# A graph layer on one core: tiles in two stretches a pair, and node spans a pair later

## The chip, the cores and the metric

The kernel runs on one core of a Trainium2 chip. The metric is the device time of one execution in microseconds. The kernel before was timed in three runs: 3030.13, 3025.53 and 3028.81 us, a median of 3028.81.

## The reference

A layer of a graph network with 12,500 nodes of 32 features and 400,000 edges, sorted by their target node `dst`:

```python
h = relu(layernorm(x))
e = concat([h[src], h[dst], edge_attr])          # 96 features an edge
v = relu(e @ W1 + b1) @ W2 + b2                  # 96 -> 64 -> 32
cand = segment_max(v, dst, num_segments=12500)   # the largest v of each node's edges
out = x + maximum(cand, h)
```

All is float32.

## The kernel before

**Tiling.** The edges are cut into four stripes of 100,000; each stripe takes 32 of the 128 partitions. A stripe is cut into chunks of 512 edges, 196 chunks in all (`NCH`), so one chunk holds 4 x 512 edges. The main loop handles two chunks a turn, called a **pair** here: `for c in range(0, NCH, 2)`, with `a = c + 2` and `b = c + 3` the next two chunks, which are prepared while c and c + 1 are finished.

**A chunk.** The hidden layer is a sum of three products in PSUM (`ph`): the edges' own features (`edges_into`, from the load `ea`), the target nodes' part (`windows_into`, a small window `qw` of precomputed rows times a one-hot `of` that `window_hots` makes on ACT out of the load `db`), and the source nodes' part (`ht`, from `h[src]`).

Source rows come in two ways. Twelve of the sixteen groups of 128 rows of a chunk are fetched by indirect DMAs on POOL (`gather`, L159, one DMA a group), and DVE transposes them in four parts (`to_features(c, 0..3)`, L274). The other four groups are taken by TensorE out of a copy of all rows on chip (`tile(c, m)`, L256: 14 matmuls of 448 columns with a one-hot `hot`, then two DVE operations that pick the row, L260 and L261). `to_features(c, J)` transposes those. The one-hots `hot` of a chunk are made by DVE (`one_hots`, groups 0 to 4, L225) and ACT (`one_hots_act`, groups 5 and 6, L234 and L235) from the load `kb`; `mask_of` belongs to them.

After `ph` come the bias and relu on ACT (`hid`, L574), the second layer on PE (into `pv`, L591), and a running maximum along the edges on DVE (`sm`, a scan that starts anew at each node, L598; the load `pb` tells it where). The last edge of each node then holds the node's maximum. To bring these to memory, `leave_1` transposes a chunk's `sm` on PE (four matmuls, L500) and adds `b2` on DVE (`so`, L502); `lasts` makes a one-hot of the last edges on DVE (L492); `leave_2` multiplies both on PE (L510), copies the result to `wo` on ACT (L514), and SP stores four windows of 32 nodes (L518).

**Order.** The order of the instructions on SP, PE, DVE and ACT is that of the program, written out by hand. In a pair it is: tile(a,0); the `ht` matmuls; `hid`; tile(a,1) and tile(a,2), with the one-hots of b between them on DVE; `ea`, second layer and window matmuls; `leave_2` of the chunk c - 1; the two scans; tile(a,3); `leave_1(c)`; tile(b,0); `leave_2(c)`; tile(b,1); `leave_1(c + 1)`; tile(b,2), tile(b,3). So PE does the tiles in stretches of 3 (b,2, b,3 and the next a,0), 2, 1, 1 and 1.

**Loads.** Each fourth chunk `load` brings `ea` (1 MB, issued on SP), `db` (1 MB) and `pb` (0.5 MB, both issued on ACT) for four chunks; the pairs between bring `kb` on ACT. Each pair SP also issues eight small loads `qw`. Waits for PSUM: the tag `pv` has three buffers, which tiles, second layer, transposes and `leave_2` share in the order of the program.

After the loop the stores are read back, the maximum with `h` and the sum with `x` are made on DVE, and the result is stored.

Of the kernel before, what the change touches and what calls it, by code (L numbers as in the profile page):

```python
# [8 lines left out]
F32 = mybir.dt.float32  # L9
# [5 lines left out]
ALU = mybir.AluOpType  # L15
# [8 lines left out]
P = 128  # L24
N = 12500
E = 400000
D = 32
# [40 lines left out]
def gnn_kernel(ctx, tc, x, src, src_mm, src_t, dst, dst_ext, lo, lo_c, ends_b, edge_attr, weights, w1, w2, b2, out):  # L68
# [84 lines left out]
    def gather(c):  # L153
        n = min(K - MM * (c in MMC), (SE - c * C) // D)
        parts = []
        for k in range(0, n, SOME):
            parts.append(gathered.tile([P, SOME, D], F32, name="gh"))
            for i in range(min(SOME, n - k)):
                nc.gpsimd.indirect_dma_start(  # L159
                    out=parts[-1][:, i, :], out_offset=None, in_=h_d[:, :],  # L160
                    in_offset=bass.IndirectOffsetOnAxis(ap=src_i[:, c, k + i:k + i + 1], axis=0))
        return parts
# [82 lines left out]
    def tile(c, m):  # L245

        if c not in MMC:
            return
        if m == 0:
            mm_rows[c] = early.tile([P, MM, D], F32, name="gm", bufs=6)  # L250
        hot = hots[c]
        e = slice(m * P, (m + 1) * P)
        po = early_ps.tile([P, C], F32, name="pv", bufs=3)[:, :D * A0]
        for k in range(A1):
            for part in range(2):
                nc.tensor.matmul(po, hot[:, k, e], hs[:, part, k].rearrange("p f a -> p (f a)"),  # L256
                                 start=(k == 0 and part == 0), stop=(k == A1 - 1 and part == 1))
        of_group = po.rearrange("p (f a) -> p f a", a=A0)
        one = early.tile([P, D, A0], F32, name="one", bufs=2)
        nc.vector.tensor_tensor(one, of_group, masks[c][:, m, None, :].to_broadcast([P, D, A0]), op=ALU.mult)  # L260
        nc.vector.tensor_reduce(mm_rows[c][:, m, :], one, axis=AX.X, op=ALU.max)  # L261

    def to_features(c, part):

        if c >= NCH:
            return
        if c not in hts:
            hts[c] = early.tile([P, K, D], F32, name="ht", bufs=4)
        ht = hts[c]
        n = min(K - MM * (c in MMC), (SE - c * C) // D)  # L270
        if part < J:
            r = slice(part * SOME, min((part + 1) * SOME, n))
            if r.start < n:
                nc.vector.transpose(ht[:, r].rearrange("p k e -> p (k e)"),  # L274
                                    gh[c][part][:, :r.stop - r.start].rearrange("p k f -> p (k f)"))
# [31 lines left out]
    with tc.tile_pool(name="nodes", bufs=1) as pool, tc.tile_pool(name="nodes_ps", bufs=2, space=PSUM) as ps:  # L307
# [147 lines left out]
    with tc.tile_pool(name="edges", bufs=3) as pool, tc.tile_pool(name="edges_ps", bufs=1, space=PSUM) as ps:  # L455
# [46 lines left out]
            nc.vector.tensor_tensor(so, px, b2r[:, None, :].to_broadcast([P, J, P]), op=ALU.add)  # L502
            return so

        def leave_2(c, so, last):

            pw = early_ps.tile([P, C], F32, name="pv", bufs=3)[:, :2 * D]
            for j in range(J):
                for g in range(2):
                    nc.tensor.matmul(pw[g * 2 * W:(g + 1) * 2 * W],  # L510
                                     last[:, j, 2 * g:2 * g + 2].rearrange("p s w -> p (s w)"),
                                     so[:, j, g * 2 * D:(g + 1) * 2 * D], start=(j == 0), stop=(j == J - 1))
            wo = pool.tile([P, 2 * D], F32, name="wo")
            nc.scalar.activation(wo, pw, AF.Copy)  # L514
            _, base = windows.pop(c)
            for s in range(NS):
                g = slice(s * W, (s + 1) * W)
                nc.sync.dma_start(top_d[s % 2][bass.ds(base[s], W), :], wo[g, s % 2 * D:(s % 2 + 1) * D])  # L518

        def into_ph(ph, pairs, start, stop):  # L520
            for s in range(NS):
# [25 lines left out]
        windows_into(0, ph)  # L547
        raw_2(3)
        raw_3(3)
        sm = None  # L550
        leave = lambda: None
        for c in range(0, NCH, 2):
            a, b = c + 2, c + 3
            for k in range(a, min(a + 2, NCH)):
                gh[k] = gather(k)
            load_keys(a + 2)
            for k in range(c + AHEAD, min(c + AHEAD + 2, NCH)):
                load(k)
            b_next = (c + 3 * AHEAD) // BLOCK
            if c % LOAD and b_next < NB and b_next not in ats and b_next not in loaded_b:  # L560
                load_block(b_next)

            if a == NCH - 2:
                nc.gpsimd.tensor_tensor(again.rearrange("p (g a) f -> p g a f", a=A0),
                                        hs[:, 0].rearrange("p g f a -> p g a f"),
                                        hs[:, 1].rearrange("p g f a -> p g a f"), op=ALU.add)
            tile(a, 0)
            to_features(a, 0)
            ht = [hts.pop(c + x).rearrange("p k e -> p (k e)") for x in range(2)]
            into_ph(ph, [(w1a, ht[x]) for x in range(2)], False, True)  # L570
            hid = []
            for s in range(NS):
                hid.append(pool.tile([P, C], F32, name="hid", bufs=6))
                nc.scalar.activation(hid[s], ph[s], AF.Relu, bias=b1c)  # L574
            for k in range(a, min(a + 2, NCH)):
                window_hots(k)
            one_hots_act(b)
            one_hots(b, 0, 2)
            tile(a, 1)
            to_features(a, 1)  # L580
            one_hots(b, 2, BY_ACT.start)
            mask_of(b)
            tile(a, 2)
            to_features(a, 2)
            last = [lasts(c)]
            ph = edges_into(a)
            pv = [early_ps.tile([P, C], F32, name="pv", bufs=3) for x in range(2)]
            for s in range(NS):
                for x in range(2):
                    g = slice(x * HID, (x + 1) * HID)  # L590
                    nc.tensor.matmul(pv[x][s * D:(s + 1) * D], w2x[g], hid[s][g], start=True, stop=True)  # L591
            windows_into(a, ph)
            leave()
            sms = []
            for x in range(2):
                before = -LOW if sm is None else sm[:, C - 1:C]
                sm = pool.tile([P, C], F32, name="sm", bufs=3)
                nc.vector.tensor_tensor_scan(sm, loaded.pop(c + x)[2], pv[x], before, op0=ALU.add, op1=ALU.max)  # L598
                sms.append(sm)
            tile(a, 3)  # L600
            one_hots_act(a + 2)
            to_features(a, 3)
            to_features(a, J)
            so = leave_1(c, sms[0])
            last.append(lasts(c + 1))
            tile(b, 0)
            to_features(b, 0)
            one_hots(a + 2, 0, 2)
            leave_2(c, so, last[0])
            tile(b, 1)  # L610
            to_features(b, 1)
            so = leave_1(c + 1, sms[1])
            one_hots(a + 2, 2, BY_ACT.start)
            mask_of(a + 2)
            tile(b, 2)
            to_features(b, 2)
            if c == 2 * AHEAD:
                places(FIRST, len(MMC))
            if (c + 4) % BLOCK == 0 and (c + 4) // BLOCK < NB:
                make_block((c + 4) // BLOCK)  # L620
            tile(b, 3)
# [12 lines left out]
            leave = lambda c=c + 1, so=so, last=last[1]: leave_2(c, so, last)  # L634
        leave()


    with tc.tile_pool(name="out", bufs=1) as pool:
# [152 lines left out]
```

## Time and profile before

| | |
|---|---|
| median of 3 runs | 3028.81 us |
| the profiled execution | 3030.95 us, its span 3029.2 us |
| PE matmul busy | 2886.8 us (95%) |
| POOL busy | 2242.3 us (74%), 2321 gathers of 944 ns |
| DVE busy | 2237.1 us (74%) |
| ACT busy | 1084.6 us (36%) |
| granted TensorE clock | 0.982 |

The profile is of one execution. A row of the timeline has the start and the length in us, the engine, the line, the operation, what it writes and reads, and how many were merged; in brackets stand the idle time of the engine before it and what ended it. A row of a group has the count, then the busy time in us and the mean of one in ns, then the idle time of the engine just before these instructions and what ended most of it. An engine's name with a q is its sequencer, which issues DMAs. Issuing a DMA isn't counted as busy, except for the indirect ones on POOL.

### The profile page before, as it was taken

What the parts mean: (1) busy time and instruction counts of PE and PEld (TensorE: products, weight loads), DVE (VectorE), ACT (ScalarE), POOL (GpSimd) and SP (SyncE); (2) the same over time, 40 slices, a digit from 0 to 9 for tenths busy, and PEclk for the clock granted to TensorE, in tenths of its full rate; (3) what the DMA queues carried; (4) which work ended last, traced back from release to release, by engine and by line L of the source; (5) the groups of instructions that cost most, each with busy time, mean ns of one, the idle gap of its engine ahead of it and who ended that gap; (6) DMA issues with size and microseconds to landing.
All of it is one profiled execution on the core that took longest, in us unless ns stands there. A gap on an engine that the chain in (4) does not pass through costs nothing. (4 is left out here: it accounts for less than half of the span.)

```text
span 3029.2 us, 58575 instructions
## 1 busy us (share of the span) xinstructions
PE 2886.8 (95%) x21077; PEld 2303.5 (76%) x21077; DVE 2237.1 (74%) x3865; ACT 1084.6 (36%) x1791; POOL 2242.3 (74%) x2372
## 2 busy tenths in 40 slices
PE   2899999999999999999999999999999999999995
PEld 1678787787878878787878787878787878787774
DVE  5578777777777777777777777777777777777775
ACT  3343433334343343434343434343434343334341
POOL 7777777777777777777777777777777777777774
PEclk7899999999999999999999999999999999999997
DMA  5432233233324323332333233223332332223322
GB/s 200 120 84 71 63 81 79 63 66 84 73 59 86 77 60 75 81 70 60 67 83 72 60 69 84 69 63 66 84 73 59 70 83 70 63 66 82 70 54 72
DMA packets 189045, 229.43 MB, mean 76 GB/s; under 512 B 117821, under 2 KB 160461, under 8 KB 175950
## 3 DMA queue, kind: packets, MB, share of 16 engines
q10 hardware_dynamic: 26692, 110.28, 12.1%
q1 hardware_dynamic: 86762, 76.66, 10.9%
q0 software_dynamic: 75296, 38.70, 8.9%
q8 instruction: 166, 2.72, 0.4%
q14 instruction: 129, 1.06, 0.1%
HBM read 211.54 MB, written 13.85 MB: 74 GB/s over the span
## 5 line engine op out<-in xcount | busy, mean ns | idle before, releaser
L159 POOL DMA_INDIRECT gh<-h_d,src_i x2321 | 2192.1, 944 | 740.6 <-issue 527.7
L256 PE MATMUL pv<-hs,hot 128*128 128x448 f32 x10808 | 2304.3, 368 | 40.8 <-DVE sm L598 40.8
L256 PEld LDWEIGHTS pv<-hs,hot 128*128 128x128 f32 x10808 | 1999.4, 189 | 266.3 <-issue 69.0
L260 DVE TENSOR_TENSOR one<-pv,mask 128x448 f32<-128x448 f32 x772 | 478.1, 619 | 629.4 <-PE pv L256 629.4
L574 ACT ACTIVATE hid<-ph,wt 128x512 f32<-128x512 f32 x392 | 237.2, 688 | 1240.7 <-PE ph L524 1099.6
L225 DVE TENSOR_TENSOR hot<-kb,consts 128x1024 fp32r<-128x1024 f16 (+2 forms) x385 | 561.0, 1457 | 0.0
L261 DVE TENSOR_REDUCE gm<-one 128x32 f32<-128x448 f32 x772 | 478.6, 620 | 26.6
L235 ACT ACTIVATE hot<-away,ones 128x512 fp32r<-128x512 f32 x386 | 279.3, 723 | 274.6 <-issue 261.7
L234 ACT ACTIVATE away<-kb,key_n 128x512 f32<-128x512 f16 x386 | 273.6, 709 | 0.0
L598 DVE TENSOR_TENSOR_SCAN sm<-pb,sm,pv 128x512 f32<-128x512 bf16 x195 | 247.6, 1270 | 17.3 <-PE pv L591 5.9
L274 DVE STREAM_TRANSPOSE ht<-gh 128x96 f32<-128x96 f32 x774 | 208.4, 269 | 58.7 <-DMA gh<-h_d,src_i 58.2
L510 PEld LDWEIGHTS pv<-so,last 128*64 128x64 f32 x3136 | 108.1, 138 | 114.5 <-DVE last L492 86.1
L514 ACT ACTIVATE wo<-pv 128x64 f32<-128x64 f32 x196 | 44.0, 224 | 344.1 <-PE pv L510 307.1
L486 ACT ACTIVATE of<-db,below 128x512 f32<-128x512 int32 x196 | 141.5, 722 | 24.8 <-DMA db<-in_dst_ext 24.8
L487 ACT ACTIVATE of<-of,ones 128x512 f32<-128x512 f32 x196 | 141.9, 724 | 6.4
L510 PE MATMUL pv<-so,last 128*64 128x64 f32 x3136 | 135.2, 229 | 5.2 <-DVE so L502 4.0
L524 PE MATMUL ph<-of,qw 32*64 32x512 f32 x1568 | 114.1, 617 | 21.1 <-DMA qw<-q_d 21.1
L524 PE MATMUL ph<-ea,wt 32*64 32x512 f32 x1568 | 110.0, 617 | 21.5 <-DMA qw<-q_d 21.5
L492 DVE TENSOR_TENSOR last<-consts,at 128x512 f32<-128x512 f32 x196 | 129.9, 663 | 0.0
L502 DVE TENSOR_TENSOR so<-pv,wt 128x512 f32<-128x512 f32 x196 | 127.8, 652 | 2.2 <-PE pv L500 2.2
L500 PE MATMUL pv<-ident,sm 128*128 128x128 f32 x784 | 118.1, 273 | 0.8 <-DVE sm L598 0.8
L524 PE MATMUL ph<-ht,wt 32*64 32x512 f32 x1568 | 116.0, 617 | 0.0
(80 smaller groups left out, 590.7 us busy)
## 6 DMA issues: line engine op xcount, KB each, us to landing
ea<-in_edge_attr SPq DMA_DIRECT2D x49, 1024.0 KB
db<-in_dst_ext ACTq DMA_DIRECT2D x48, 1024.0 KB
gh<-h_d,src_i POOLq DMA_INDIRECT x2321
pb<-pen_d ACTq DMA_DIRECT2D x48, 512.0 KB
kb<-key_d ACTq DMA_DIRECT2D x47, 512.0 KB
qw<-q_d SPq DMA_DIRECT2D x784, 8.0 KB
top_d<-wo SPq DMA_DIRECT2D x784, 4.0 KB
top_d<-zero ACTq DMA_DIRECT2D x2, 1568.0 KB
```

Of the source, the lines that this page charges most:

```text
L159: nc.gpsimd.indirect_dma_start(out=parts[-1][:, i, :], out_offset=None, in_=h_d[:, :], in_offset=bass.IndirectOffsetOnAxis(ap=src_i[:, c, ...
L225: nc.vector.tensor_tensor(hot_of(c)[:, start:stop], keys[c][:, None, :].to_broadcast([P, n, MM * P]), key_ps[:, start:stop, None].to_broad ...
L234: nc.scalar.activation(away, keys[c], AF.Square, bias=key_n[:, k:k + 1])
L235: nc.scalar.activation(hot_of(c)[:, k], away, AF.Relu, bias=ones, scale=-1.0)
L256: nc.tensor.matmul(po, hot[:, k, e], hs[:, part, k].rearrange("p f a -> p (f a)"), start=(k == 0 and part == 0), stop=(k == A1 - 1 and par ...
L260: nc.vector.tensor_tensor(one, of_group, masks[c][:, m, None, :].to_broadcast([P, D, A0]), op=ALU.mult)
L261: nc.vector.tensor_reduce(mm_rows[c][:, m, :], one, axis=AX.X, op=ALU.max)
L274: nc.vector.transpose(ht[:, r].rearrange("p k e -> p (k e)"), gh[c][part][:, :r.stop - r.start].rearrange("p k f -> p (k f)"))
L510: nc.tensor.matmul(pw[g * 2 * W:(g + 1) * 2 * W], last[:, j, 2 * g:2 * g + 2].rearrange("p s w -> p (s w)"), so[:, j, g * 2 * D:(g + 1) * ...
L524: nc.tensor.matmul(ph[s][x * HID:(x + 1) * HID], w[g], e[g], start=start, stop=stop)
L574: nc.scalar.activation(hid[s], ph[s], AF.Relu, bias=b1c)
L598: nc.vector.tensor_tensor_scan(sm, loaded.pop(c + x)[2], pv[x], before, op0=ALU.add, op1=ALU.max)
```

## The change

- The order of the tiles. `tile(a, 0)` is done at the end of the turn before. Behind the `ht` matmuls stands only tile(a,1); tile(a,2), tile(a,3), the four tiles of b and the next tile(a,0) follow the scans in one stretch. So there are two stretches, of 1 and of 7 tiles.
- `leave_1` and `leave_2` of the chunks c and c + 1 are done in the next turn: both transposes behind the `ht` matmuls, both products behind the window matmuls, in one PSUM tile with one copy `wo` and eight stores. After the loop the last two chunks are done alone.
- On DVE, both `lasts` stand behind the eviction of tile(a,1), and the one-hots 2 to 4 of chunk b behind that of tile(a,2).
- `gather` and `window_hots` of the next pair stand at the end of the turn. So does the sum `again` on POOL, one turn earlier in the program, behind the same gathers.
- `hid` has four buffers instead of six.

```diff
-        def leave_2(c, so, last):
-            pw = early_ps.tile([P, C], F32, name="pv", bufs=3)[:, :2 * D]
-            for j in range(J):
-                for g in range(2):
-                    nc.tensor.matmul(pw[g * 2 * W:(g + 1) * 2 * W],
-                                     last[:, j, 2 * g:2 * g + 2].rearrange("p s w -> p (s w)"),
-                                     so[:, j, g * 2 * D:(g + 1) * 2 * D], start=(j == 0), stop=(j == J - 1))
-            wo = pool.tile([P, 2 * D], F32, name="wo")
+        def leave_2(c, sos, last):
+            pw = early_ps.tile([P, C], F32, name="pv", bufs=3)[:, :4 * D]
+            for x in range(2):
+                for j in range(J):
+                    for g in range(2):
+                        nc.tensor.matmul(pw[g * 2 * W:(g + 1) * 2 * W, x * 2 * D:(x + 1) * 2 * D],
+                                         last[x][:, j, 2 * g:2 * g + 2].rearrange("p s w -> p (s w)"),
+                                         sos[x][:, j, g * 2 * D:(g + 1) * 2 * D], start=(j == 0), stop=(j == J - 1))
+            wo = pool.tile([P, 4 * D], F32, name="wo")
             nc.scalar.activation(wo, pw, AF.Copy)
...
+        for k in range(2, 4):
+            gh[k] = gather(k)
+            window_hots(k)
+        tile(2, 0)
+        to_features(2, 0)
...
         for c in range(0, NCH, 2):
             a, b = c + 2, c + 3
-            for k in range(a, min(a + 2, NCH)):
-                gh[k] = gather(k)
             load_keys(a + 2)
...
-            tile(a, 0)
-            to_features(a, 0)
             ht = [hts.pop(c + x).rearrange("p k e -> p (k e)") for x in range(2)]
             into_ph(ph, [(w1a, ht[x]) for x in range(2)], False, True)
             hid = []
             for s in range(NS):
-                hid.append(pool.tile([P, C], F32, name="hid", bufs=6))
+                hid.append(pool.tile([P, C], F32, name="hid", bufs=4))
                 nc.scalar.activation(hid[s], ph[s], AF.Relu, bias=b1c)
-            for k in range(a, min(a + 2, NCH)):
-                window_hots(k)
             one_hots_act(b)
             one_hots(b, 0, 2)
+            so = [leave_1(c - 2 + x, sms[x]) for x in range(2)] if c else []
             tile(a, 1)
             to_features(a, 1)
-            one_hots(b, 2, BY_ACT.start)
-            mask_of(b)
-            tile(a, 2)
-            to_features(a, 2)
-            last = [lasts(c)]
+            last = [lasts(c - 2 + x) for x in range(2)] if c else []
             ph = edges_into(a)
...
             windows_into(a, ph)
-            leave()
+            if c:
+                leave_2(c - 2, so, last)
             sms = []
...
+            tile(a, 2)
+            to_features(a, 2)
+            one_hots(b, 2, BY_ACT.start)
+            mask_of(b)
             tile(a, 3)
             one_hots_act(a + 2)
             to_features(a, 3)
             to_features(a, J)
-            so = leave_1(c, sms[0])
-            last.append(lasts(c + 1))
             tile(b, 0)
             to_features(b, 0)
             one_hots(a + 2, 0, 2)
-            leave_2(c, so, last[0])
             tile(b, 1)
             to_features(b, 1)
-            so = leave_1(c + 1, sms[1])
             one_hots(a + 2, 2, BY_ACT.start)
             mask_of(a + 2)
...
+            for k in range(a + 2, min(a + 4, NCH)):
+                gh[k] = gather(k)
+                window_hots(k)
...
             tile(b, 3)
             to_features(b, 3)
             to_features(b, J)
+            tile(a + 2, 0)
+            to_features(a + 2, 0)
...
-        leave()
+        so = [leave_1(NCH - 2 + x, sms[x]) for x in range(2)]
+        leave_2(NCH - 2, so, [lasts(NCH - 2 + x) for x in range(2)])
```

More of the change, by code (lines that the diff above doesn't have):

```diff
@@ L503, in leave_1 @@
             return so
-        def leave_2(c, so, last):
-            pw = early_ps.tile([P, C], F32, name="pv", bufs=3)[:, :2 * D]
-            for j in range(J):
-                for g in range(2):
-                    nc.tensor.matmul(pw[g * 2 * W:(g + 1) * 2 * W],
-                                     last[:, j, 2 * g:2 * g + 2].rearrange("p s w -> p (s w)"),
-                                     so[:, j, g * 2 * D:(g + 1) * 2 * D], start=(j == 0), stop=(j == J - 1))
-            wo = pool.tile([P, 2 * D], F32, name="wo")
[L514 to L518, printed above, removed]
+        def leave_2(c, sos, last):
[7 more added lines that the diff above has]
+            wo = pool.tile([P, 4 * D], F32, name="wo")
+            nc.scalar.activation(wo, pw, AF.Copy)
+            for x in range(2):
+                _, base = windows.pop(c + x)
+                for s in range(NS):
+                    g = slice(s * W, (s + 1) * W)
+                    nc.sync.dma_start(top_d[s % 2][bass.ds(base[s], W), :],
+                                      wo[g, (2 * x + s % 2) * D:(2 * x + s % 2 + 1) * D])
         def into_ph(ph, pairs, start, stop):
@@ L549, in gnn_kernel @@
         raw_3(3)
+        for k in range(2, 4):
[3 more added lines that the diff above has]
+        to_features(2, 0)
         sm = None
-        leave = lambda: None
+        sms = []
         for c in range(0, NCH, 2):
             a, b = c + 2, c + 3
-            for k in range(a, min(a + 2, NCH)):
-                gh[k] = gather(k)
             load_keys(a + 2)
@@ L561, in gnn_kernel @@
                 load_block(b_next)
[L563 to L566, printed above, removed]
-            tile(a, 0)
-            to_features(a, 0)
             ht = [hts.pop(c + x).rearrange("p k e -> p (k e)") for x in range(2)]
@@ L620, in gnn_kernel @@
                 make_block((c + 4) // BLOCK)
+            for k in range(a + 2, min(a + 4, NCH)):
+                gh[k] = gather(k)
+                window_hots(k)
+            if a + 2 == NCH - 2:
+                nc.gpsimd.tensor_tensor(again.rearrange("p (g a) f -> p g a f", a=A0),
+                                        hs[:, 0].rearrange("p g f a -> p g a f"),
+                                        hs[:, 1].rearrange("p g f a -> p g a f"), op=ALU.add)
             tile(b, 3)
@@ L633, in gnn_kernel @@
                 nc.vector.tensor_copy(general_i, bp)
-            leave = lambda c=c + 1, so=so, last=last[1]: leave_2(c, so, last)
-        leave()
+        so = [leave_1(NCH - 2 + x, sms[x]) for x in range(2)]
+        leave_2(NCH - 2, so, [lasts(NCH - 2 + x) for x in range(2)])
     with tc.tile_pool(name="out", bufs=1) as pool:
```

## The prediction

> **What bounds the kernel now.** I read the stretches first: the windows view, cut where the first wait of TensorE inside the loop over pairs appears (1211.8 us) and at the last full pair (2971.2 us).
>
> ```profile
> 92.00:1211.80 1119.80, 1119.80 (x8206) 898.12 (x8206) 855.09 (x1483) 413.60 (x683) 837.16 (x887) 1.00 0.32 73
> 1211.80:2971.20 1759.40, 1714.96 (x12531) 1374.51 (x12530) 1308.43 (x2265) 631.45 (x1044) 1314.13 (x1394) 0.99 0.31 70
> ```
>
> The columns are the length, then the busy time of PE, PEld, DVE, ACT and POOL. In the first stretch PE has no gap. In the second it lacks 44.4 us. So one thing ends the time of a pair at first and another later. The timeline of PE gives a pair in which PE never waits:
>
> ```profile
> 1546.35 1.11 PE L524 MATMUL ph<-ht,wt 32*64 32x512 f32 x16
> 1547.39 5.88 PE L256 MATMUL pv<-hs,hot 128*128 128x448 f32 x28
> 1553.20 1.11 PE L524 MATMUL ph<-ea,wt 32*64 32x512 f32 x16
> 1554.24 1.09 PE L591 MATMUL pv<-hid,wt 64*32 64x512 f32 x16
> 1555.26 1.11 PE L524 MATMUL ph<-of,qw 32*64 32x512 f32 x16
> 1556.31 0.69 PE L510 MATMUL pv<-so,last 128*64 128x64 f32 x16
> 1556.92 3.08 PE L256 MATMUL pv<-hs,hot 128*128 128x448 f32 x14
> 1559.84 0.60 PE L500 MATMUL pv<-ident,sm 128*128 128x128 f32 x4
> 1560.19 3.06 PE L256 MATMUL pv<-hs,hot 128*128 128x448 f32 x14
> 1563.18 0.69 PE L510 MATMUL pv<-so,last 128*64 128x64 f32 x16
> 1563.80 3.08 PE L256 MATMUL pv<-hs,hot 128*128 128x448 f32 x14
> 1566.71 0.60 PE L500 MATMUL pv<-ident,sm 128*128 128x128 f32 x4
> 1567.07 8.66 PE L256 MATMUL pv<-hs,hot 128*128 128x448 f32 x42
> 1575.66 0.69 PE L524 MATMUL ph<-ht,wt 32*64 32x512 f32 x8
> ```
>
> From start to start a pair takes 1575.66 - 1546.35 = 29.31 us. Now the gathers on POOL, grouped over the loop, and over two short windows that I need below (94 to 142.4 us and 142.5 to 201 us), and DVE's transposes of what they fetched:
>
> ```profile
> L159 POOL DMA_INDIRECT gh<-h_d,src_i x2311 | 2181.6, 944 | 737.7 <-issue 524.8 <-DMA gh<-h_d,src_i 117.2 <-DVE one L260 22.3
> L159 POOL DMA_INDIRECT gh<-h_d,src_i x39 | 36.8, 944 | 11.9 <-issue 10.4 <-DMA gh<-h_d,src_i 0.9 <-DVE one L260 0.3
> L159 POOL DMA_INDIRECT gh<-h_d,src_i x47 | 44.4, 944 | 15.7 <-issue 9.8 <-DMA gh<-h_d,src_i 4.3 <-DVE one L260 1.3
> L274 DVE STREAM_TRANSPOSE ht<-gh 128x96 f32<-128x96 f32 x774 | 208.4, 269 | 58.7 <-DMA gh<-h_d,src_i 58.2
> ```
>
> The second row is the floor: 0.944 busy and 11.9 / 39 = 0.305 idle, so a gather every 1.249 us. A pair has 24 gathers: 24 x 1.249 = 29.98 us, more than PE's 29.31. POOL starts with a lead, PE eats it at 0.67 us a pair, and from 1211.8 us on PE waits, by way of DVE, whose transposes stood 58.2 us in all behind gathers that hadn't landed. The second stretch holds 58 pairs: 1759.4 / 58 = 30.33 us each, POOL's floor and 0.35 more. So **the end is set by POOL's 2311 gathers**, not by PE, though PE is the busiest engine. The 0.35 is in the first row: 737.7 - 2311 x 0.305 = 32.8 us of idle time over the floor. That is the one piece of the loop that this change could win.
>
> Where it comes from: the third row has 15.7 - 47 x 0.305 = 1.4 us over the floor and the second has none. Both windows begin with a group of loads. The timelines of ACT and SP, and the list of issues, tell the difference:
>
> ```profile
> 93.88 0.61 ACTq L468 DMA_DIRECT2D db<-in_dst_ext  x1
> 93.89 0.42 SPq L465 DMA_DIRECT2D ea<-in_edge_attr  x1
> 1563.91 0.23 ACT L514 ACTIVATE wo<-pv 128x64 f32<-128x64 f32 x1 [1.73 <-PE pv L510]
> 1563.92 0.56 ACTq L468 DMA_DIRECT2D db<-in_dst_ext  x1
> 1564.16 8.77 SPq L518 DMA_DIRECT2D top_d<-wo  x4
> 1572.98 0.50 SPq L465 DMA_DIRECT2D ea<-in_edge_attr  x1
> 1574.25 19.61 SPq L480 DMA_DIRECT2D qw<-q_d  x8
> 1534.75 8.11 SPq L518 DMA_DIRECT2D top_d<-wo  x8
> db<-in_dst_ext ACTq DMA_DIRECT2D x48, 1024.0 KB
> ```
>
> At 93.9 us db and ea are issued together and POOL loses nothing. In the loop db goes out at 1563.92, behind the second wo, and ea 9.06 us later, because SP must first issue the four stores of that wo. Ea then lands on top of db, both of 1 MB, the gathers in flight are held back, and POOL, which waits for an older gather before it issues a new one, stops. Spread over 46 later loads this is 32.8 / 46 = 0.71 us each.
>
> **The change part by part.** Times t are from the start of the ht matmuls of a pair.
>
> *PE order.* Five stretches of tiles become two (14 and 98 matmuls); the four transposes of each chunk and the two groups L510 stand together. The number of matmuls is the same. A tile inside a stretch costs 8.59 / 3 = 2.86 us. A tile alone costs 2.92 before transposes, 2.99 before L510, and two cost 5.81 before ea. So a boundary costs 0.06, 0.13 or 0.09. Gone are two of the first kind and one of the second, 0.25 us; the eight transposes behind ht are a new one, between nothing and 0.13. Pair: 29.31 - 0.25 + 0.06 = 29.1, with ends 29.0 and 29.3 (none gained). That is under POOL's 29.98 at both ends, so for the sum it is worth **nothing**: POOL hides it.
>
> The Trainium skill, "TensorE: Matmul & The Clock Gate", Part 3 (packing small matmuls), says that a weight load overlaps running matmuls only when it uses other rows of the array. By that rule each of the six boundaries that go would show a whole load, and the pair would come out well below 29.0. The 0.06 to 0.13 above speak against it; the sum would be the same by both, and only rival 2 would have more room.
>
> *Moved on SP and ACT: the term that decides.* One line tells an ACT activation of this size:
>
> ```profile
> L235 ACT ACTIVATE hot<-away,ones 128x512 fp32r<-128x512 f32 x386 | 279.3, 723 | 274.6 <-issue 261.7 <-PE pv L256 3.5
> ```
>
> The two wo become one, at t = 1.04 (ht) + 0.70 (transposes) + 2.9 (tile) + 3.1 (ea, hid, of) + 1.2 (L510 twice) = 9.0. Its eight stores then go out in a row: 8.11 us by the row at 1534.75, so ea follows at t = 17 instead of 26.6 (1572.98 - 1546.35). On ACT the window one-hots (four activations) now stand behind the one-hots of the next chunk, which wait for tile(a,3) at t = 14.8: 14.8 + 3 x 0.72 + 4 x 0.72 = 19.9. The loads db and pb are queued behind, at t = 20 instead of 17.6. So **ea goes 3 us ahead of db** where it was 9 us behind. The nearest row is the one at 93.9 us: nothing lost. Bounds: all 32.8 us won, or none. I take 28 won, since some loads will fall badly.
>
> *Waits added.* ACT's window one-hots now need the db of their own iteration, issued 26 us before; queued behind are the next load and hid, for which PE waits. SP's qw loads, some of which wait for db and pb to land, are through at 1574.25 + 19.61 = 1593.9, 30 us behind db's issue, and db is the first of the two; ACT has from t = 20 to t = 30 free. Nothing, or up to 2 us a load if db is late. The gathers are written one iteration earlier in the program but POOL has nothing else in its queue: no change, and `again` stays behind the last of them.
>
> *DVE.* The same operations in another order. Two lasts, and the scans behind them, stand straight behind the eviction of tile(a,1):
>
> ```profile
> L260 DVE TENSOR_TENSOR one<-pv,mask 128x448 f32<-128x448 f32 x772 | 478.1, 619 | 629.4 <-PE pv L256 629.4
> L261 DVE TENSOR_REDUCE gm<-one 128x32 f32<-128x448 f32 x772 | 478.6, 620 | 26.6
> L225 DVE TENSOR_TENSOR hot<-kb,consts 128x1536 fp32r<-128x1536 f16 x192 | 331.3, 1726 | 0.0
> L492 DVE TENSOR_TENSOR last<-consts,at 128x512 f32<-128x512 f32 x196 | 129.9, 663 | 0.0
> L502 DVE TENSOR_TENSOR so<-pv,wt 128x512 f32<-128x512 f32 x196 | 127.8, 652 | 2.2 <-PE pv L500 2.2
> L598 DVE TENSOR_TENSOR_SCAN sm<-pb,sm,pv 128x512 f32<-128x512 bf16 x195 | 247.6, 1270 | 17.3 <-PE pv L591 5.9
> 1527.61 3.08 PE L256 MATMUL pv<-hs,hot 128*128 128x448 f32 x14 [0.79 <-DVE sm L598]
> ```
>
> Tile(a,1) ends at t = 4.7; evicted and rows transposed (0.62 + 0.62 + 0.2) at 6.3; lasts at 7.6; first scan at 8.9, when PE arrives at tile(a,2), which needs its buffer, at 9.0. One-hots 2 to 4 of chunk b are ready at 12.1 + 1.4 + 1.7 = 15.2; tile(b,0) needs them in its fifth matmul, at 14.8 + 4 x 2.86 / 14 = 15.6. Both fit with a few tenths to spare, as the scan did before (a late gather made it 0.79 us late in the last row). Cost nothing; without that cover, what it lacks, each pair.
>
> *End.* The tail has no tiles to hide behind. The rows are from PE, ACT and the critical chain:
>
> ```profile
> 2988.53 3.24 PE L524 MATMUL ph<-ht,wt 32*64 32x512 f32 x16
> 3003.62 0.22 ACT L514 ACTIVATE wo<-pv 128x64 f32<-128x64 f32 x1 [2.73 <-PEq L644]
> 3009.37 4.54 DMA acc<-top_d
> ```
>
> From the last ht to the last wo: 15.1 us; from there to the end of the stores and the reload 5.7. After the change eight transposes stand before the last scans (+1), the two lasts behind the so (+1.3), one L510 round is saved (-1.5), and eight stores instead of four follow the last wo (+4 by 8.11 / 8). Sum **+5**, between 2 and 9.
>
> **Sum.** -28 + 5 = -23 us. The profiled execution took 3030.95 us (span 3029.2 and 1.75 around it), 2.1 above the median of 3028.81. 3028.81 - 23 = **3006 us**. Bounds: -32.8 + 2 gives 2998, and a pair of PE that comes closer to POOL at the end can give another 4.
>
> **The rivals.** (1) *The order of the loads doesn't matter.* Their bytes are the same, POOL's 32.8 us stay, the tail is added: 3028.8 + 5 = 3034 us (3028 to 3038). Against it: the window at 94 us. For it: that window is a single one, at the start. The Trainium skill, "DMA: Bandwidth & Descriptors", section "Issuing engines are not separate DMA queues", says that transfers from all queues run on the same 16 engines and interleave whichever engine starts them; read so, this is what happens.
>
> (2) *DVE's order makes PE the bound, slower.* If the scan, the lasts or the one-hots of tile(b,0) come late, every pair pays. The 96 pairs of the two windows now take 2879.2 us, 29.99 each, with POOL's lead included. My forecast leaves (2879.2 - 28) / 96 = 29.7 us a pair, so it decides from 0.6 us of stall a pair on; at 1.4 us of stall (30.5) the time is 3028.8 + 96 x 0.51 + 5 = 3083, at 1.0 us (30.1) 3044. For it: slack of 0.1 to 0.4 us in three places. Against: each is a matter of tenths, and DVE is idle for a quarter of the time (1308.43 of 1759.40 busy).
>
> (3) *It does what it says and POOL stops half as often*: -16 + 5, 3018.
>
> **How the numbers follow.** A measurement of this kernel tells about 0.2% (6 us) from no change: faster is under 3022.8, slower over 3034.9. Forecast 0.50, rival 3 0.12, rival 1 0.20 (about half inside the 0.2%, half above), rival 2 0.18 (nearly all above). Faster 0.62, same 0.12, slower 0.26. The range goes from 2994 (all won, PE closer at the end) to 3040, which holds rival 1 and leaves out most of rival 2 and little below. The forecast's own range is 2994 to 3016.
>
> **What would show it.** Right: POOL's idle time per gather near 0.305 throughout, a total under 715 us; ea ahead of db in each load; a pair of PE without waits near 29.1; PE waiting more in total and still ending earlier; 5 us more from the last ht to the reload. Wrong: POOL's idle time still near 738 (rival 1); PE waiting for DVE sm, last or hot in every pair from the first on, with POOL's gathers waiting for DVE ht because the buffers are full (rival 2); hid waiting behind window one-hots.

## The result, and the profile after

The changed kernel took 2999.65 us (median of 6, 2996.32 to 3000.29) where the kernel before, run beside it, took 3028.36 (median of 6, 3025.34 to 3030.13): a ratio of 0.9907, 95% interval 0.9895 to 0.9918. That is 28.7 us less; forecast were 23. Ratios, here and below, are of undisturbed executions alone and so differ a little from the quotient of the medians. All experiments further down ran on chips on which the kernel before took 4060 to 4104 us (medians) and the change cost time (1.0251, interval 1.0182 to 1.0320), so no time from there may be set against the 3000 of here; what holds the kernel up there is part of what they showed.

The windows of the profiled execution of after, cut about where TensorE's pairs begin to wait and at the last full pair:

```profile
92.00:1160.00 1068.00, 1067.05 (x7930) 868.64 (x7930) 826.85 (x1431) 397.19 (x629) 807.69 (x855) 1.00 0.31 75
1160.00:2940.80 1780.80, 1750.94 (x12784) 1412.13 (x12782) 1334.19 (x2314) 632.62 (x1003) 1345.98 (x1425) 0.99 0.29 70
```

The last full pair begins at 2940.8 us where it began at 2971.2. TensorE (first busy column) still lacks 29.9 us in the second stretch: it still waits for POOL. The groups, POOL's over the loop and then from the whole span:

```profile
L159 POOL DMA_INDIRECT gh<-h_d,src_i x2310 | 2184.6, 946 | 704.9 <-issue 526.3 <-DMA gh<-h_d,src_i 104.7 <-DVE one L260 16.8
L274 DVE STREAM_TRANSPOSE ht<-gh 128x96 f32<-128x96 f32 x774 | 208.2, 269 | 109.4 <-DMA gh<-h_d,src_i 109.4
```

POOL's idle time over its floor is 704.9 - 2310 x 0.305 = 0.35 us; it was 32.8. The second row is VectorE standing behind gathers that haven't landed: 109.4 us, up from 58.2. The kernel waits more for gathers and ends earlier, because TensorE has become quicker than POOL by more. The two queues that load, around one group of loads:

```profile
1538.72 6.97 SPq L520 DMA_DIRECT2D top_d<-wo  x8
1545.73 0.42 SPq L465 DMA_DIRECT2D ea<-in_edge_attr  x1
...
1548.38 0.56 ACTq L468 DMA_DIRECT2D db<-in_dst_ext  x1
```

Ea goes out 2.65 us ahead of db here, and ahead of it in every one of the 47 loads that follow the first (median 3.5 us); it was 9.1 us behind. And a pair of TensorE without a wait:

```profile
645.23 1.11 PE L527 MATMUL ph<-ht,wt 32*64 32x512 f32 x16
646.27 1.09 PE L500 MATMUL pv<-ident,sm 128*128 128x128 f32 x8
647.12 3.06 PE L256 MATMUL pv<-hs,hot 128*128 128x448 f32 x14
650.11 1.11 PE L527 MATMUL ph<-ea,wt 32*64 32x512 f32 x16
651.15 1.09 PE L586 MATMUL pv<-hid,wt 64*32 64x512 f32 x16
652.17 1.11 PE L527 MATMUL ph<-of,qw 32*64 32x512 f32 x16
653.22 1.15 PE L511 MATMUL pv<-so,last 128*64 128x64 f32 x32
654.30 19.88 PE L256 MATMUL pv<-hs,hot 128*128 128x448 f32 x98
674.11 1.25 PE L527 MATMUL ph<-ht,wt 32*64 32x512 f32 x16
```

674.11 - 645.23 = 28.88 us, against 29.31. So TensorE's own work got 0.43 us a pair shorter, some 41 us over 96 pairs, and this didn't set the end: 24 gathers take 29.98.

**Where the 31.2 us of the two spans (3029.2 and 2998.0) come from**, along POOL: 32.5 us less held up, 3.9 us more busy (2311 gathers of 946 in place of 944 ns; the row above leaves out the last one), and 0.5 us from an earlier start of the loop's gathers, so the last gather starts 29.1 us earlier (2951.97, from 2981.04). From there to the last ht matmuls it is 5.5 us in place of 7.5, and from those to the end 40.5 in place of 40.7.

**What held POOL up in before** can be read gather by gather. A gather starts on POOL, and the events of its semaphore tell when it landed. The gathers use eight semaphores in turn and each waits for its own, that is, for the gather 8 back. In before 75 gaps between gathers are more than 0.05 us over the floor, 33.0 us together. All of them lie 1.6 to 18.6 us after the issue of an ea (11 to 28 us after that of its db), and 68 of them, 25.6 us, end within 0.8 us of the landing of the gather 8 back (the other 7 within 1.7 to 3.7 us). In after there are 3 such gaps, 0.7 us together.

### The profile page after: what moved, and what is told of

Read it like the earlier page. It is cut to its first block, busy times and chain, and to the rows that moved or that the text cites. A ratio compares the mean times of both kernels' runs of the same rounds, so it can differ in the third digit from the quotient of the medians.

```text
span 2998.0 us, 58325 instructions
## 1 busy us (share of the span) xinstructions
PE 2868.3 (96%) x21077; PEld 2312.6 (77%) x21077; DVE 2237.3 (75%) x3865; ACT 1068.6 (36%) x1693; POOL 2245.8 (75%) x2372
## 5 line engine op out<-in xcount | busy, mean ns | idle before, releaser
L256 PE MATMUL pv<-hs,hot 128*128 128x448 f32 x10808 | 2219.5, 364 | 0.9 <-DVE sm L594 0.9
L256 PEld LDWEIGHTS pv<-hs,hot 128*128 128x128 f32 x10808 | 2016.7, 188 | 143.4 <-issue 3.2
L274 DVE STREAM_TRANSPOSE ht<-gh 128x96 f32<-128x96 f32 x774 | 208.2, 269 | 109.4 <-DMA gh<-h_d,src_i 109.4
L527 PE MATMUL ph<-ht,wt 32*64 32x512 f32 x1568 | 142.1, 640 | 25.1 <-DVE ht L277 25.1
L511 PEld LDWEIGHTS pv<-so,last 128*64 128x64 f32 x3136 | 100.1, 138 | 80.4 <-PE pv L586 74.7
L500 PEld LDWEIGHTS pv<-ident,sm 128*128 128x128 f32 x784 | 89.5, 147 | 85.3 <-issue 70.8
L515 ACT ACTIVATE wo<-pv 128x128 f32<-128x128 f32 x98 | 27.3, 278 | 298.1 <-PE pv L511 286.5
L492 DVE TENSOR_TENSOR last<-consts,at 128x512 f32<-128x512 f32 x196 | 122.5, 663 | 0.0
L511 PE MATMUL pv<-so,last 128*64 128x64 f32 x3136 | 113.7, 226 | 1.4 <-DVE last L492 1.4
```

The source lines that it names most:

```text
L511: nc.tensor.matmul(pw[g * 2 * W:(g + 1) * 2 * W, x * 2 * D:(x + 1) * 2 * D], last[x][:, j, 2 * g:2 * g + 2].rearrange("p s w -> p (s w)"), ...
L527: nc.tensor.matmul(ph[s][x * HID:(x + 1) * HID], w[g], e[g], start=start, stop=stop)
```

## The experiments

**Theory 1**: the time was won by the order of two loads; ea behind db held up gathers, and POOL, which doesn't issue a gather before the one 8 back has landed, stopped. **Theory 2**: it was won by TensorE's longer stretches. Each kernel was timed beside the kernel before on its chip.

*Ea ahead of db in the kernel before.*

```
 def load(c, queue=nc.scalar):
-    ea = pool.tile(...); nc.sync.dma_start(ea[:, :n], ea_v[:, c * C:c * C + n])
+    ea = early_ea.pop(c) if c in early_ea else load_ea(c)
 ...
 windows_into(a, ph)
 leave()
+if (c + 2) % LOAD == 0 and c + 2 + AHEAD < NCH:
+    early_ea[c + 2 + AHEAD] = load_ea(c + 2 + AHEAD)
```

> The kernel before with one edit: the load of ea is issued on SP half a pair earlier, right behind the first four stores (about t = 13 of the pair), so that it goes out some 4.6 us ahead of db (t = 17.6) where it went out 9.06 us behind it. PE, DVE, ACT and POOL keep their order. Theory 1 (the change won by the order of the two loads): POOL's idle time over its floor of 0.305 us a gather falls from 32.8 us to 0 to 4, and the time to 2996 to 3002 us. Theory 2 (the change won by the longer stretches of tiles, a pair of 28.88 us in place of 29.31): PE's order is the one of before, so the time stays at 3026 to 3031.

> The kernel e1_before_ea_ahead once more, after a run in which the kernel before took some 4065 us and POOL waited for TensorE in every pair, so that the loads could not hold up anything. Where the kernel before takes 3026 to 3031 us: theory 1, ea ahead of db alone brings POOL's idle time over its floor from 32.8 us to 0 to 4 and the time to 2996 to 3002 us; theory 2, it stays at 3026 to 3031, since PE's order is that of before.

*Ea behind db in the kernel after.*

```
 windows[c] = qw, bases.pop(c)
+if c % LOAD == 0 and queue is nc.scalar:
+    nc.sync.dma_start(ea[:, :n], ea_v[:, c * C:c * C + n])
```

(and in the loop not in its old place ahead of db).

> The kernel after with one edit: the load of ea is issued on SP behind the four qw loads of its first chunk, about 10 us later than now, so some 7 us behind db where it went out 3.7 us ahead of it. Theory 1: POOL is held up again by 0.5 to 0.7 us a load, its idle time over the floor is 20 to 33 us, and the time 3020 to 3033. Theory 2: the stretches of tiles are untouched, 2998 to 3002 us and nothing over the floor.

> The kernel e2_after_ea_behind once more, for the same reason. Where the kernel before takes 3026 to 3031 us: theory 1, POOL is held up again by 0.5 to 0.7 us a load, 20 to 33 us over its floor, and the time is 3020 to 3033 us; theory 2, it keeps the 2998 to 3002 of the kernel after, since the stretches of tiles are untouched.

*Db and pb in four DMAs of 32 partitions, in the kernel before.*

```
-queue.dma_start(db[:, :n], ap(dst_ext, 1 + c * C, [[S, NS], [0, D], [1, n]]))
+for s in range(NS):
+    queue.dma_start(db[s * D:(s + 1) * D, :n], ap(dst_ext, 1 + c * C + s * S, [[0, D], [1, n]]))
```

(pb alike).

> The kernel before with db and pb each loaded by four DMAs of 32 partitions in place of one of 128; same bytes, same queue, ea still 9 us behind db. In the trace of before the bytes of db and pb move at about 4 us of engine time per us for 20 us, those of ea at 15. Theory 1 in the form that ea and db must not share the few engines that carry db: if the four DMAs spread over all engines, db and pb are through in 6 to 8 us, before ea is issued, POOL's idle time over the floor is 0 to 6 us and the time 2996 to 3004. In the form that what holds the gathers up is the order alone, or the sum of bytes within some 20 us: 25 to 45 us over the floor, 3020 to 3040. Theory 2: 3026 to 3031.

*Ea on ACT between db and pb, in the kernel before.*

```
 queue.dma_start(db[:, :n], ...)
+queue.dma_start(ea[:, :n], ea_v[:, c * C:c * C + n])
 queue.dma_start(pb[:, :n], ...)
```

(and in the loop no longer on SP).

> The kernel before with ea issued on ACT directly behind db (0.6 us) and ahead of pb, in place of 9.06 us behind db on SP. Theory 1 in the form that whatever comes behind db stacks on it: 25 to 40 us over POOL's floor, 3020 to 3035 us. In the form that ea harms only when it meets db in mid-flight from another queue (at 93.9 us of the kernel before both went out together and nothing was lost): 0 to 6 us over the floor, 2996 to 3004. Theory 2: 3026 to 3031.

The times decided none of these expectations:

| kernel | us, median | before beside it | ratio, 95% interval |
|---|---|---|---|
| e1_before_ea_ahead | 4035.99 | 4064.90 | 0.9887, 0.9823 to 0.9952 |
| e1r (the same) | 4063.81 | 4104.32 | 0.9935, 0.9851 to 1.0019 |
| e2_after_ea_behind | 4205.59 | 4064.90 | 1.0338, 1.0254 to 1.0422 |
| e2r (the same) | 4220.66 | 4104.32 | 1.0313, 1.0230 to 1.0397 |
| e3_before_stripes | 4068.58 | 4064.90 | 1.0004, 0.9959 to 1.0050 |
| e4_before_ea_with_db | 4106.40 | 4064.90 | 1.0094, 1.0038 to 1.0150 |

Here a pair took about 40 us, and POOL wasn't the bound; its waits in e1r:

```profile
POOL gh L159 <- DVE ht L274: 693.7, 259, 15.5
POOL gh L159 <- issue: 589.7, 1881, 5.3
POOL gh L159 <- DVE ht L277: 362.4, 94, 10.8
```

1056 us behind VectorE's transposes, that is, for buffers to come free. What the loads hold up there can hide in pauses that POOL makes anyway, so the premise of all these expectations was missing. Of the times only e1's leans theory 1's way, by 1%, and its repetition has an interval that holds 1.

*More gathers, to make POOL the bound there too.*

```
-parts.append(gathered.tile([P, SOME, D], F32, name="gh"))          # 18 buffers
-for i in range(min(SOME, n - k)):
+parts.append(gathered.tile([P, SOME + MORE, D], F32, name="gh"))   # MORE = 2, 11 buffers
+for i in range(SOME + MORE if c in MMC else min(SOME, n - k)):
```

> The kernel before with 20 gathers a chunk in place of 12: every tile of gh gets two more columns, gathered and never read, and 11 such tiles in place of 18. POOL then takes 40 x 1.249 = 49.96 us a pair, more than TensorE needs on any chip seen here, so that POOL is the bound throughout and whatever holds its gathers up shows in the time. Loads and stores are those of before. Some 3855 gathers: 62.9 + 3845 x 1.249 + 46 = 4911 us if nothing holds them up. Theory 1: ea is issued 9 us behind db, POOL's idle time over its floor (0.305 us a gather) is 25 to 40 us, the time 4935 to 4950 us. Theory 2: the loads hold nothing up that counts, or it is the same in all four kernels of this series.

> As d1_before_20, with the one edit of e1_before_ea_ahead: ea goes out on SP behind the first four stores, ahead of db. Theory 1: 0 to 5 us over POOL's floor, 25 to 35 us less time than d1_before_20. Theory 2: as d1_before_20.

> The kernel after with the same 20 gathers a chunk. Theory 1: 0 to 5 us over POOL's floor, and the time of d2_before_ea_ahead_20 within 5 us, since PE's order is covered by POOL in both. Theory 2: less than d2_before_ea_ahead_20 by what the longer stretches win.

> As d3_after_20, with the one edit of e2_after_ea_behind: ea goes out on SP behind the first chunk's four qw loads, some 7 us behind db. Theory 1: 20 to 40 us over POOL's floor, 20 to 35 us more time than d3_after_20. Theory 2: as d3_after_20.

They took 6217.95, 6217.58, 6511.07 and 6523.54 us (medians of 4; 6197.81 to 6295.21, 6154.81 to 6271.66, 6497.28 to 6569.43, 6516.46 to 6566.09). All four expectations of some 4911 to 4950 us missed, by a quarter to a third: with 16 more gathers a pair took not 50 but 62 to 66 us, and POOL still waited for VectorE. The kernel after was to take what d2 takes, within 5 us, and took 293 more. In d4_after_ea_behind_20 ea stayed ahead of db in most loads (median 2.9 us), so its time tested nothing. What POOL lost to gathers not landed does follow the order, in little: d1, then d2:

```profile
POOL gh L160 <- DMA gh<-h_d,src_i: 23.6, 68, 1.1
```

```profile
POOL gh L160 <- DMA gh<-h_d,src_i: 14.0, 46, 0.3
```

(Total, times, longest.) 23.6 - 68 x 0.305 = 2.9 us over the floor with ea behind, 14.0 - 46 x 0.305 = 0.0 with ea ahead.

**The trace decides what the times could not.** How long a gather takes from its start to its landing can be worked out on any chip. POOL issues every 1.249 us and waits for the gather 8 back, so a gather that takes longer than 8 x 1.249 = 9.99 us stops a POOL that issues without pause; in before the stops begin at some 9.3 us, since the next gather starts 0.26 to 0.74 us behind the landing. Counted from the traces:

```
kernel                   ea issued after db   gathers over 9 us   over 10 us
before                        +9.1 us               310               92
after                         -3.5                   11                0
e1_before_ea_ahead, e1r       -2.9, -3.0           1, 1             0, 0
a0_after (below)              -3.4                    8                0
e2_after_ea_behind, e2r       +1.8, +1.7          63, 53           25, 11
e4_before_ea_with_db          +0.6                   54               12
e3_before_stripes             +5.3                    0                0
d1_before_20                  +9.1                  184               62
d2_before_ea_ahead_20         -4.9                    3                0
d3_after_20                   -5.2                   24               15
d4_after_ea_behind_20         -2.8                   33               15
```

(Medians over some 48 loads each; TensorE's order is that of before in e1, e3, e4, d1, d2.) The median hides loads that went the other way: in e2 and e2r ea was to go out 7 us behind db, and went out more than 0.5 us behind it in 28 and 25 of 48 loads; in d3 it was behind in 3 loads, in d4 in 7. Load by load, over all these kernels but e3: of 345 loads with ea more than 0.5 us ahead of db, none had a gather over 9.99 us; of 207 with ea more than 0.5 us behind, 81 had (in before 24 of 47). All 15 slow gathers of d3, and of d4, fall to loads with ea behind. With TensorE's order as it was, moving ea alone takes the slow gathers away (d1 to d2, on one chip, 62 to 0; before's 92 were counted on another chip than e1's 0), and with TensorE's new order, moving ea back brings them again. That is theory 1. Half a microsecond behind is enough, on db's own queue too (10 of 48 loads in e4), though 9 us did it more often (19 of 48 in d1).

e3 tells what it is about the order. In before, counted by packets, db and then pb keep about 4 us of DMA engine time busy per us, for more than 20 us. Ahead of db, in after, ea keeps up to 16 busy and is through in some 5 us; behind db, in before, it keeps 7 to 12 busy for 6 us and then some 2 for 6 more, as if its share on db's engines came late. The issues of one load in e3, of ACT and SP:

```profile
2020.15 6.16 ACTq L469 DMA_DIRECT2D db<-in_dst_ext  x4
2026.29 0.42 SPq L465 DMA_DIRECT2D ea<-in_edge_attr  x1
```

Three of db's four DMAs go out within 1 us and keep 14 to 15 busy for 3 us; the fourth goes out 0.4 us ahead of ea. All of db is through 7.5 us after its first issue (median), some 0.6 us after ea's first packet began. Ea is still issued behind db, and its beginning still meets db's last quarter, but the longest gather of the kernel takes 6.1 us. So it isn't order as such: **what holds the gathers up is a load on few engines for long with another issued behind it**. That the gathers' own shares wait on just those engines is argued, since the trace doesn't tell which engine moved a packet. Ahead of db, ea is nearly gone when db starts. The Trainium skill, "DMA: Bandwidth & Descriptors", section "Why a DMA increments its semaphore by 16 and not by 1" (how many engines), says that a DMA uses the largest number of engines up to 16 that divides the slowest dimension of both sides. By that it is 4 for db, whose source has 4 stripes, and 16 for a DMA of 32 rows; the trace agrees, with the 4 and the 14 to 15 counted.

*The change itself on these chips.*

> The kernel after, unchanged, beside the kernel before. In the experiments so far the kernel before took about 4060 us, TensorE stood still for some 12 us in each pair with no wait that the profile shows while POOL gathered, and POOL waited for TensorE. If that is so here too: theory 1 says that the order of the loads can win nothing then, and only TensorE's new order counts; from e2_after_ea_behind (3 per cent over before) and from d3_after_20 against d1_before_20 (4.7 per cent) the time is 4150 to 4230 us. Theory 2 (longer stretches are what wins): under 4040 us. If the kernel before takes 3026 to 3031 us here: 2997 to 3002 us by both.

4191.98 us against 4096.36: 1.0251. This is as theory 1 expected: with POOL not the bound, the order of the loads wins 1% at most (e1 and e1r above), and theory 2's longer stretches win nothing either. A pair takes 41.5 us (median) where it takes 39.9 in e1r. TensorE's waits in a0_after:

```profile
PE ph L527 <- issue: 217.4, 214, 20.9
PE pv L256 <- DVE hot L225: 125.9, 90, 1.4
PE pv L256 <- DVE one L260: 65.6, 78, 1.7
```

and in e1r, with the order of before:

```profile
PE ph L531 <- issue: 146.1, 144, 19.3
PE pv L256 <- issue: 122.5, 198, 1.9
PE pv L256 <- DVE one L260: 83.3, 83, 1.3
```

The row on hot is new: 1.4 us in 90 of the pairs, beside the 1.6 by which a pair is longer. That it is the main part is argued, since other rows differ too (issue before L256 is 88.6 us less, issue before the ph matmuls 71.3 more). It is of the kind of the prediction's rival 2, in another place: all 90 stand before the fifth matmul of tile(a+2,0), the last tile of the long stretch. The timelines of PE, DVE and POOL in a0_after, one after the other, show it:

```profile
2020.21 17.08 PE L256 MATMUL pv<-hs,hot 128*128 128x448 f32 x84
2038.91 1.08 PE L256 MATMUL pv<-hs,hot 128*128 128x448 f32 x4 [1.62 <-DVE one L260]
2041.39 2.28 PE L256 MATMUL pv<-hs,hot 128*128 128x448 f32 x10 [1.39 <-DVE hot L225]
```

```profile
2030.32 1.18 DVE L225 TENSOR_TENSOR hot<-kb,consts 128x1024 fp32r<-128x1024 f16 x1
2038.23 0.62 DVE L260 TENSOR_TENSOR one<-pv,mask 128x448 f32<-128x448 f32 x1 [6.74 <-PE pv L256]
...
2039.62 1.72 DVE L225 TENSOR_TENSOR hot<-kb,consts 128x1536 fp32r<-128x1536 f16 x1
```

```profile
2025.06 0.94 POOL L159 DMA_INDIRECT gh<-h_d,src_i  x1 [4.27 <-DVE ht L274]
...
2035.31 0.94 POOL L159 DMA_INDIRECT gh<-h_d,src_i  x1 [0.30 <-issue]
2039.97 0.94 POOL L159 DMA_INDIRECT gh<-h_d,src_i  x1 [3.72 <-DVE ht L274]
```

VectorE stands still for 6.74 us up to 2038.23. The row names PE, but PE works through 84 matmuls, six tiles, from 2020.21 to 2037.29, and the fourth of these tiles, the next for VectorE, was done at 2031.69: VectorE had work and did not start it. POOL gathered from 2025.06 to 2036.25 without a pause; 2 us after it stopped VectorE goes on, evicts late, makes the one-hots late, and TensorE waits 1.39 us for them in the last tile of its stretch. That TensorE loses more in the new order because a stretch of 98 matmuls gives VectorE nowhere to catch up is argued from this picture, not shown.

*Without the gathers.*

```
 parts.append(gathered.tile([P, SOME, D], F32, name="gh"))
+if c in MMC:
+    nc.gpsimd.memset(parts[-1], 0.0)
+    continue
```

> The kernel after without the gathers of its loop: each tile of gh is set to zero by POOL, so the sums over gathered rows of h are left out; loads, stores, tiles and the order of every other engine stay. In the experiments so far TensorE starts some 7 matmuls a us when POOL has just begun to gather and about 1 a us once it has gathered for more than 12 us in a row. Theory 3 (the gathers starve TensorE's issue there, and this is why the change lost): without them a pair takes the 28.88 us of the change's own trace from the first to the last, 97 + 27 + 95 x 28.88 + 57 + 9 = 2925 to 2945 us. Rival (TensorE is slow there by itself): 3900 to 4200 us.

2936.18 us (2932.26 to 2937.39) on a chip where the kernel before takes 4070.21: inside the 2925 to 2945 of theory 3. Its windows and a stretch of TensorE's timeline:

```profile
92.00:1160.00 1068.00, 1068.00 (x7937) 869.85 (x7937) 827.90 (x1433) 397.27 (x630) 52.49 (x294) 1.00 0.20 62
1160.00:2870.00 1710.00, 1707.84 (x12761) 1394.12 (x12760) 1329.79 (x2308) 632.57 (x1003) 98.80 (x466) 1.00 0.19 59
```

```profile
1513.10 1.11 PE L530 MATMUL ph<-ht,wt 32*64 32x512 f32 x16
1514.14 1.09 PE L503 MATMUL pv<-ident,sm 128*128 128x128 f32 x8
1514.99 3.06 PE L259 MATMUL pv<-hs,hot 128*128 128x448 f32 x14
```

TensorE lacks 2.2 us in 2778, the granted clock is 1.00, and a pair takes 28.91 us on average. So TensorE is not slower on this chip: what a pair loses there it loses only with the gathers in the kernel. It also prices the change's TensorE order by itself: 28.9 us a pair hold from the first to the last when nothing of POOL stands in the way, and VectorE's new order costs TensorE no wait that repeats.

## Why the prediction was right, point by point

- *POOL's gathers set the end; TensorE's order is worth nothing beside them.* Held: 28.88 us (28.91 without gathers) against POOL's 29.98, and from 62.5 to 2952 us POOL makes no pause over 0.8 us, so nothing that TensorE does could have ended the gathers much earlier. The pair was forecast at 29.1, ends 29.0 and 29.3; the change gave 0.43 us, not 0.19. The seven tiles of the long stretch take 674.11 - 654.30 = 19.81 us, 2.83 each, and the 2.86 forecast for a tile "inside a stretch" had the boundary of a stretch of three still in it. The eight transposes take 0.85 us in place of 0.71, the products 1.08 in place of 1.23. It didn't matter for the sum.
- *The term that decides, ea against db: -28.* Measured -32.5, close to the whole 32.8 that was its bound. Ea was forecast at t = 17 and db at t = 20; they go out at about t = 15 to 17 and at t = 19.1 to 20.1. The reason given was right in direction and is now shown by loads; it was incomplete, since "both of 1 MB" isn't what counts but the few engines of db. The later loads are 47, not 46. The 4.8 us kept back for "loads that fall badly" had no ground: no load did.
- *POOL's floor.* 3.9 us were given back by gathers of 946 in place of 944 ns, which the sum didn't have.
- *Waits added on ACT and SP, and VectorE's slack of some tenths: nothing.* Held on this chip: TensorE's tiles wait 0.9 us in all for a scan (it was 40.8), and none of the waits forecast as possible repeats in the loop. On the other chips none of the three covers that were counted failed, but one that the prediction didn't look at: the one-hots of tile(a+2,0). In the pair of after above they are ready at 668.92 and used at 672.01, 3.1 us later; a VectorE that stands still for 6.74 us uses that up.
- *The tail: +5, between 2 and 9.* This is the term that was mis-sized: it is about 0 (40.7 to 40.5 us from the last ht to the end). The rows of after, of PE, ACT and SP:

```profile
2957.50 1.78 PE L527 MATMUL ph<-ht,wt 32*64 32x512 f32 x16 [1.75 <-DVE ht L277]
...
2960.23 2.63 PE L586 MATMUL pv<-hid,wt 64*32 64x512 f32 x16
...
2969.72 0.28 ACT L515 ACTIVATE wo<-pv 128x128 f32<-128x128 f32 x1 [5.46 <-PE pv L511]
...
2978.18 2.05 SPq L725 DMA_DIRECT2D acc<-top_d  x4
```

From the last ht to the last wo it is 12.2 us, where 15.1 + 0.8 were forecast; from there to the reload 8.5, where 5.7 + 4 were. So both halves were sized too long, by 3.7 and 1.3 us. Most of the 3.7 goes with the clock. The windows from the last ht to the end of the second layer, in before and then in after (the third number from the end is the granted clock):

```profile
2988.50:2996.10 7.60, 6.87 (x35) 1.32 (x35) 1.59 (x3) 2.42 (x4) 7.57 (x1) 0.55 0.02 2
2957.50:2962.90 5.40, 5.40 (x43) 1.95 (x45) 3.08 (x8) 2.42 (x4) 5.40 (x1) 1.00 0.00 0
```

The prediction sized its tail on rows of which the first, of the ht matmuls, had run at a granted clock of 0.55. In after it was still 1.00 there: the ht matmuls took 1.78 us in place of 3.24 and the second layer 2.63 in place of 3.61, so the stretch is 2.2 us shorter although eight transposes were put into it. Why the clock fell earlier in before's tail is not known.
- *Closer to POOL at the end: up to 4.* 2.0 us, from the last gather to the last ht.

Sum by the spans: -32.5 + 3.9 - 0.5 - 2.0 - 0.2 = -31.3, beside the -31.2 of the two profiled executions. The forecast of -23 fell short because its two terms were both too cautious, the loads by 4.5 us and the tail by 5; the gathers' longer time took part of that back. The medians differ by 28.7: before's profiled execution (3030.95 us) lay 2.6 over its median, after's (2999.86) 0.2.

Of the rivals, 1 (the order of the loads doesn't matter) falls by the count over 552 loads, and 3 (half) by POOL's 0.35 us. Rival 2 did not come on the chip that was predicted for. On the others VectorE's one-hots did come late, at 1.4 us a pair, but not those of tile(b,0) and not for want of a few tenths. That ea's order alone, without TensorE's new order, gives 3000 us where before takes 3028 was not measured: no run fell on such a chip.

## What to carry to other kernels

Find the engine whose instructions have no slack and ask what else stops *it*; here a gain of 0.43 us a pair on the busiest engine was worth nothing, and having one 1 MB load issued ahead of another ended stops of POOL worth 1%. Where gathers are in flight, look for a bulk load that uses few DMA engines and has another issued right behind it; here issuing the other ahead, or cutting the first so that it spreads, ended the slow gathers. And a schedule's slack is worth what the disturbances leave of it: the same change won 0.9% on a chip where TensorE kept its pace beside the gathers and lost 2.5% on one where it didn't.

## What the runs showed of the hardware that was not expected

On the chips of the experiments, TensorE slows down while POOL gathers. Counted in e1r from the moment POOL starts a row of gathers, TensorE starts 7 to 9 matmuls a us in the first two us, 4.5 in the eleventh and 1.0 in the fourteenth; in d1_before_20, where POOL can go on for longer, 0.5 to 0.9 from the 16th us on. POOL's timeline of d1 and below it TensorE's:

```profile
3011.30 0.95 POOL L160 DMA_INDIRECT gh<-h_d,src_i  x1 [0.30 <-issue]
3025.75 0.95 POOL L160 DMA_INDIRECT gh<-h_d,src_i  x1 [13.50 <-DVE ht L278]
...
3006.44 1.01 PE L525 MATMUL ph<-of,qw 32*64 32x512 f32 x1 [1.09 <-issue]
3008.54 1.01 PE L525 MATMUL ph<-of,qw 32*64 32x512 f32 x1 [1.09 <-issue]
3010.64 1.01 PE L525 MATMUL ph<-of,qw 32*64 32x512 f32 x1 [1.09 <-issue]
3012.04 1.86 PE L525 MATMUL ph<-of,qw 32*64 32x512 f32 x2 [0.40 <-issue]
3014.84 3.38 PE L525 MATMUL ph<-of,qw 32*64 32x512 f32 x6 [0.94 <-issue]
```

One matmul in 2.1 us, with no wait that the profile shows, until some 3 us after POOL's pause began at 3012.25. On the chip of the result POOL gathered for up to 360 us with no pause over 0.8 us, and in before TensorE started 4 to 15 matmuls a us in the same count. The packets that the trace shows (gathers, loads, instructions) are no slower on the one than on the other: 1.1 us for 16 KB of instructions on both. That the slowing goes with the gathers is shown by f1_after_no_gathers, which leaves them out; what they block, and why not on the chip of the result, stays open.
